# A transformer block with adaptive layer norm: one MLP part moved to the end of the program, bias sums tile by tile, and a second way to empty a PSUM bank

## The chip, the cores and the metric

The kernel runs on one core of one Trainium2 chip. The metric is the device time of the whole program in microseconds (us), lower is better. Engines are named as in the profile: PE is TensorE, DVE is VectorE, ACT is ScalarE, POOL is GpSimd, SP is the engine that issues most DMAs.

## The reference, cut to what matters

The input x has 8 sequences of 1024 tokens with 512 channels, all in float32. From a condition vector come six rows per sequence: shift, scale and gate for attention and for the MLP.

```python
mod = silu(condition) @ Wada + bada
sh_a, sc_a, gt_a, sh_m, sc_m, gt_m = jnp.split(mod, 6, axis=1)
xm = layernorm(x, g1, be1) * (1 + sc_a) + sh_a
x = x + gt_a * (causal_attention(xm, Wqkv, 16 heads) @ Wproj + bproj)
xm = layernorm(x, g2, be2) * (1 + sc_m) + sh_m
x = x + gt_m * (gelu(xm @ W1 + b1) @ W2 + b2)      # W1: 512 -> 2048, W2: 2048 -> 512
```

## The kernel before, in words

**Blocks.** The tokens are cut into 16 blocks of 512, numbered 0 to 15; an even block is the first half of a sequence, an odd one the second half. Attention of an odd block also looks at the keys of the even one before it, so it is about twice as long. Per block there are these steps of linear work on PE: `k`, `q`, `v` (projections), `proj` (output projection), `u` 0 to 3 (MLP up, four quarters) and `d` 0 to 3 (MLP down, four parts). All but `proj` use Strassen's seven products in place of eight. A down product is 64 matmuls, which the profile shows as 128 records; a product of the others is 32 records. Of the seven down products, parts 0 and 1 and part 3 have two each, part 2 has one. `mt` is not linear work: it normalizes the residual, turns it and writes the MLP's input `xm_m`; `at` does this for attention's input `xm_a`. In blocks 0, 1, 14 and 15 the turning is done by PE, in the others by DVE and DMA.

**One order, laid by a planner.** The kernel's Python runs once and writes every engine's instructions in order. It keeps an estimated clock for each engine in `now`, and due times of keys in `written` and `left`. Two streams are merged: attention (`attend`), and a list of linear steps, `plan[w]` for each window w, where window w runs beside attention of block w. `step_aside` inserts linear work ahead of an attention step if that step would wait by the planner's clocks, or if the linear work done is less than what is due. What is due grows with each attention step at a `rate`, which is the planned time of `plan[w]` over the need of the window's attention. `plan[16]` holds what runs when all attention has been placed. Threads started beside the main list (`start`) come first in the list of threads, and the first with the least wait is taken.

**The steps around the change.** In `plan[15]` the order is: part 1 of block 13, `proj` and `mt` of block 14, parts 2 and 3 of block 13, then the four up steps of block 14, its parts 0 and 1. `plan[16]` has part 2 of block 14, part 3 as a thread beside, then `proj`, `mt` and the MLP of block 15. `proj` waits until attention of its block is finished, and what stands behind it in the main list waits with it. In even windows the order is k, q, v of the next block.

**Banks and sums.** Linear products go to three PSUM banks. `copy_out` empties a bank by DVE or ACT, whichever is sooner by the clocks; `combine_out` adds the product to an earlier one and is always on DVE (line 193). `either` (lines 158 and 161) puts an SBUF sum on DVE or POOL by the clocks.

**The residual.** `load_xr` loads x for a block, and queues four jobs that add the bias row `gba` (gate times `bproj`) to its four tiles, in `pool_jobs`. These are placed when POOL is idle by its clock and the data is there; what is left is placed at the end of `project_out`. Then `bias_row(n, "m")` loads the row `gbm` into the same single buffer, by a DMA on SP's queue. `act_jobs` holds the four normalizing instructions of a block, placed when ACT or DVE is not ahead of PE by the clocks.

Of the kernel before, what the change touches and what calls it, by code (L numbers as in the profile page):

```python
# [12 lines left out]
ALU = mybir.AluOpType  # L13
# [9 lines left out]
def kernel(  # L23
# [33 lines left out]
    nc = tc.nc  # L57
# [6 lines left out]
    NTT = TB // P  # L64
# [47 lines left out]
    def note(engine, ns, reads=(), writes=(), port=False):  # L112
        start = max(now[engine], due(reads, writes))
        if port:
            start = max([start] + [b for a, b in pool_spans if a <= start < b])
        end = start + ns
        now[engine] = end
        if engine == "POOL":
            pool_spans.append((start, end))
            del pool_spans[:-16]  # L120
        for k in reads:
            left[k] = max(left.get(k, 0.0), end + SYNC)
        for k in writes:
            written[k] = end + SYNC
        return end
# [64 lines left out]
        live[bank] = not last  # L190

    def combine_out(out, bank, src, other, reads=(), writes=(), op=ALU.add, last=True):
        nc.vector.tensor_tensor(out, src, other, op)  # L193
        note("DVE", 690, [("l", bank), *reads], writes)
        live[bank] = not last

    def matmul(ps, lhsT, rhs, start, stop, reads=(), bank=None):
# [30 lines left out]
    def mlp_steps(n):  # L228
        return [("u", n, i) for i in range(NQ)] + [("d", n, part) for part in range(4)]
# [9 lines left out]
    for w in range(1, NB):  # L239
        n = w - 1  # L240
        m = mlp_steps(n)
        even = blocks[n][1] == 0
        rows_a = [("rows", blocks[n][0], "a")] if even else []
        rows_m = [("rows", blocks[n][0], "m")] if even else []
        own = m[:1] + ([("load_xa", w + 2)] if w + 2 < NB else []) + m[1:3]
        own += [("norm_a", w + 2)] if w + 2 < NB else []
        if w == NB - 1:
            steps = late[:1] + rows_a + [("proj", n), ("mt", n)] + late[1:]
            steps += rows_m + own + m[3:5] + [("load_xr", w)] + m[5:6]
            late = m[6:]  # L250
        else:

            steps = late + [("v", w)] + rows_a + [("proj", n), ("mt", n), ("k", w + 1)]
            if w > 3 and blocks[w][1]:
                steps = late[:-1] + rows_a + [("proj", n), ("mt", n)] + late[-1:] + [("k", w + 1)]
            if w == 2:
                steps = late + [("v", w), ("k", w + 1)] + rows_a + [("proj", n), ("mt", n)]
            if w == 1:
                steps = rows_a + [("k", w + 1), ("proj", n), ("mt", n)]
            early_v = [("v", w + 1)] if w > 2 and not blocks[w][1] else []  # L260
            steps += [("q", w + 1)] + early_v + rows_m + own
            at = [("at", w + 2)] if w + 2 < NB else []
            if blocks[w][1] == 0:

                steps += m[3:5] + [("load_xr", w)]
                late = m[5:6] + at + m[6:]
            else:
                steps += m[3:5] + [("load_xr", w)] + m[5:6] + at
                late = m[6:]
        plan[w] = steps  # L270
    n = NB - 1
    plan[NB] = [late[0], ("beside", late[1]), ("proj", n), ("mt", n)] + mlp_steps(n)

    kept_sums = {}
    column_source = {"k": (Wqkv, 1), "q": (Wqkv, 0), "v": (Wqkv, 2)}
# [265 lines left out]

    def run_act_jobs(everything=False):
        while act_jobs and (
            everything or (min(now["ACT"], now["DVE"]) <= now["PE"] and due(act_jobs[0][1]) <= now["PE"])
        ):
            act_jobs.pop(0)[0]()

# [469 lines left out]
    def add_to(xt, other, reads, writes, op=ALU.add):  # L1017
        either(xt, xt, other, op, [*reads, *writes], writes)

    def project_out(n):  # L1020
        at = take(NC)
        yield [("attended", n), ("xr begun", n)], []
        attT = qTs[n]
        tiles = [residual[n][:, t, :] for t in range(NTT)]
        last = n == NB - 1
        begun = []

        def begin(t):

            bank = yield from accumulate(  # L1030
                [(attT[:, c, ts(t, P)], piece(at[c])) for c in range(NC - 1)], [("att", n)], False
            )
            begun.append(bank)

        for t, xt in enumerate(tiles):
            if last:
                while len(begun) <= max(t, 1):
                    yield from begin(len(begun))
                bank = begun[t]
                yield [("att", n, t)], []  # L1040
                matmul(
                    banks[bank], attT[:, NC - 1, ts(t, P)], piece(at[NC - 1]), False, True,
                    [("att", n, t)], bank,
                )
            else:
                bank = yield from accumulate(
                    [(attT[:, c, ts(t, P)], piece(at[c])) for c in range(NC)], [("att", n)]
                )
            y = tmp.tile([P, D], F32, tag="y", name=f"y_{n}_{t}", bufs=2)
            ky = y_key("proj", True)  # L1050
            combine_out(y, bank, banks[bank], gate_rows["ga"], [("row", "ga")], [ky], ALU.mult)
            if last:
                run_pool_jobs(True)
                nc.vector.tensor_tensor(xt, xt, y, ALU.add)
                note("DVE", 700, [ky, ("xr", n, t)], [("xr", n, t)], port=True)
                following = normalize_tile(xt, f"m{n}", t, ("xr", n, t))
                if t > 0:
                    pending()
                pending = following
            else:  # L1060
                add_to(xt, y, [ky], [("xr", n, t)])
        if last:
            pending()
        release(*at)
        run_pool_jobs(True)
        bias_row(n, "m")
        if not last:
            normalize(residual[n], f"m{n}", [("xr", n, t) for t in range(NTT)])

    def up(step):  # L1070
        _, n, q = step

        def gelu():
            for i in range(NC):
                f = q * NC + i
                nc.scalar.activation(  # L1076
                    hT[:, i, :], hT[:, i, :], AF.Gelu, bias=cols[:, O_B1 + f : O_B1 + f + 1]
                )
                k = q // 2 + 1
                note_act(590, "gelu", [("h", n, q)], [(n, f"B{k}1"), (n, f"B{k}2"), ("g", n, q)])  # L1080

        def finished():
            if q == NQ - 1:
                written["m used", n] = 0.0
            excursion(gelu, [("h", n, q)], first=True)

        if (n, q) == (0, 0):
            yield ["prepared up"], []
        written["g", n, q] = NEVER
        hT = act.tile([P, NC, TB], F32, tag="hT", name=f"hT_{n}_{q}", bufs=NQ)  # L1090
        hTs[n, q] = hT

        yield from strassen(
            step,
            f"m{n}",
            lambda f, t: hT[:, half(f, 2), half(t, HB)],
            ("h", n, q),
            False,
            finished,
        )  # L1100
# [31 lines left out]
    def load_xr(n):  # L1132

        if n > 1:
            yield [("stored", n - 2)], []
        xr = xrp.tile([P, NTT, D], F32, tag="xr", name=f"xr_{n}")
        residual[n] = xr
        for t in range(2):
            nc.sync.dma_start(xr[:, half(t, 2), :], some_rows(x, n, t))
        for t in range(NTT):  # L1140
            written["xr", n, t] = now["PE"] + LANDING
        if n > 0:
            yield [("xr", n - 1, t) for t in range(NTT)], []
        bias_row(n, "a")
        row = ("row", "gba", n)
        for t in range(NTT):
            job = lambda t=t: add_to(xr[:, t, :], gate_rows["gba"], [row], [("xr", n, t)])
            pool_jobs.append((job, [("xr", n, t), row]))
        written["xr begun", n] = 0.0

    def down(n, part):
# [85 lines left out]
        if part == 0:  # L1237
            yield [("g", n, 0), ("g", n, 1), "prepared", ("row", "gbm", n)], []
            for i in range(NTT):
                add_to(residual[n][:, i, :], gate_rows["gbm"], [("row", "gbm", n)], [("xr", n, i)])  # L1240
            combine(nc.vector, "B12", "B12", "B11")
            bank, ps = yield from product("B11")
            got["u1"] = stage("p1", "p1")
# [24 lines left out]
        else:  # L1268
# [15 lines left out]
            store(n, 0)  # L1284
            for q in range(NQ):
                hTs.pop((n, q))


    def perform(step):
# [576 lines left out]
    for n in range(NB):  # L1866
        written["attended", n] = NEVER
        written["v done", n] = NEVER
        written["stored", n] = NEVER
        written["xr begun", n] = NEVER  # L1870
        written["m used", n] = NEVER
        if n > 1:
            written["free for v", n] = NEVER
        if n > 2:
            written["free for k", n] = NEVER
# [70 lines left out]
```

## Time and profile before

| | us |
|---|---|
| median of 3 runs | 3536.86 (3535.36 to 3538.43) |
| the profiled execution | 3537.37 |
| its span, first to last instruction | 3534.7 |
| PE busy | 3461.9 (98%) |
| DVE, POOL, ACT busy | 2201.4 (62%), 2054.0 (58%), 1208.4 (34%) |

The busy time of PE is a model: matmuls overlap, and a busy PE is not PE at its peak. The granted clock is TensorE's share of its full speed. A group's row gives the number of instructions, their busy time and the mean of one, then the idle time of that engine just before them and what ended it. `w,hT` marks down products, `xm_m,w` and `t_m,w` up products, `w,qT` the output projection, `w,xm_a` and `w,t_a` the v projection.

### The profile page before, as it was taken

What the parts mean: (1) busy time and instruction counts of PE and PEld (TensorE: products, weight loads), DVE (VectorE), ACT (ScalarE), POOL (GpSimd) and SP (SyncE); (2) the same over time, 40 slices, a digit from 0 to 9 for tenths busy, and PEclk for the clock granted to TensorE, in tenths of its full rate; (3) what the DMA queues carried; (4) which work ended last, traced back from release to release, by engine and by line L of the source; (5) the groups of instructions that cost most, each with busy time, mean ns of one, the idle gap of its engine ahead of it and who ended that gap; (6) DMA issues with size and microseconds to landing.
All of it is one profiled execution on the core that took longest, in us unless ns stands there. A gap on an engine that the chain in (4) does not pass through costs nothing. (4 is left out here: it accounts for less than half of the span.)

```text
span 3534.7 us, 120362 instructions
## 1 busy us (share of the span) xinstructions
PE 3461.9 (98%) x54429; PEld 1732.1 (49%) x54429; DVE 2201.4 (62%) x2438; ACT 1208.4 (34%) x1264; POOL 2054.0 (58%) x2228
## 2 busy tenths in 40 slices
PE   8999999999999999999999999999999999999999
PEld 4444445454454545445454444544555445554445
DVE  5776675565657666665566666665666756655463
ACT  2334323352233523335233442333423343223431
POOL 2666846566357663756727566375753658537560
PEclk9999999999999999999999999999999999999999
DMA  6753434435445445353453534545354545443334
GB/s 199 239 167 106 136 115 138 138 112 157 136 127 152 111 155 153 120 160 118 135 155 119 167 112 147 149 138 145 116 158 136 154 130 147 132 134 98 114 91 140
DMA packets 328195, 491.11 MB, mean 139 GB/s; under 512 B 27260, under 2 KB 177596, under 8 KB 324100
## 3 DMA queue, kind: packets, MB, share of 16 engines
q1 hardware_dynamic: 327568, 483.39, 46.1%
q8 instruction: 428, 7.01, 0.8%
q14 instruction: 83, 0.68, 0.1%
q10 hardware_dynamic: 116, 0.03, 0.0%
HBM read 425.57 MB, written 55.64 MB: 136 GB/s over the span
## 5 line engine op out<-in xcount | busy, mean ns | idle before, releaser
L1769 POOL TENSOR_TENSOR pT<-pT,pT 128x256 f32<-128x256 f32 (+3 forms) x1254 | 1214.4, 1003 | 330.0 <-PE po L1679 186.9
L1651 ACT ACTIVATE pT<-st 128x2048 f32<-128x2048 f32 x288 | 541.0, 1878 | 1059.3 <-PE st L1639 952.3
L202 PE MATMUL bank<-w,hT 128*32 128x256 f32 x14336 | 822.7, 380 | 0.5 <-issue 0.5
L1563 DVE TENSOR_REDUCE mx<-sc 128x4 f32<-128x2048 f32 (+3 forms) x381 | 658.9, 1750 | 228.1 <-PE sc L1548 222.3
L202 PEld LDWEIGHTS bank<-w,hT 128*32 128x32 f32 x14336 | 446.5, 110 | 392.7 <-issue 111.6
L202 PE MATMUL bank<-xm_m,w 128*32 128x256 f32 x8192 | 498.5, 382 | 1.6 <-ACT xm_m L750 0.8
L202 PE MATMUL bank<-t_m,w 128*32 128x256 f32 x6144 | 381.6, 380 | 0.6 <-DVE t_m L762 0.6
L1656 POOL TENSOR_SCALAR_AFFINE_SELECT pT<-pT 128x512 f32<-128x512 f32 x256 | 173.6, 696 | 342.3 <-ACT pT L1651 339.8
L202 PEld LDWEIGHTS bank<-xm_m,w 128*32 128x32 f32 x8192 | 256.2, 110 | 223.9 <-issue 56.4
L1560 DVE TENSOR_TENSOR sc<-sc,mask 128x1024 f32<-128x1024 f32 (+1 forms) x158 | 161.5, 1022 | 309.8 <-PE sc L1548 246.5
L1548 PE MATMUL sc<-kT,qT 32*128 32x512 f32 (+3 forms) x3048 | 329.4, 522 | 8.3 <-ACT pT L1651 4.4
L1679 PE MATMUL po<-pT,v 128*32 128x512 f32 (+3 forms) x3048 | 302.0, 491 | 3.8 <-POOL pT L1656 3.6
L1639 PE MATMUL st<-qT,kT 32*128 32x512 f32 (+3 forms) x3072 | 303.8, 488 | 0.0
L202 PEld LDWEIGHTS bank<-t_m,w 128*32 128x32 f32 x6144 | 189.4, 110 | 172.8 <-issue 46.9
L1718 DVE RECIPROCAL rec<-rec 128x128 f32<-128x128 f32 x256 | 227.3, 922 | 49.0 <-ACT rec L1709 49.0
L202 PE MATMUL bank<-xm_a,w 128*32 128x256 f32 x3968 | 241.7, 380 | 0.0
L202 PE MATMUL bank<-w,qT 128*32 128x512 f32 x2048 | 238.4, 599 | 1.1 <-DMA w<-in_L_cond_Wproj_dram 1.1
L1548 PEld LDWEIGHTS sc<-kT,qT 32*128 32x128 f32 x3048 | 130.3, 184 | 191.0 <-issue 94.4
L193 DVE TENSOR_TENSOR hT<-bank,u_u 128x512 f32<-128x512 f32 x192 | 130.4, 687 | 112.0 <-PE bank L202 108.8
L202 PE MATMUL bank<-t_a,w 128*32 128x256 f32 x2944 | 185.3, 381 | 1.4 <-DVE u_d L193 1.4
L1076 ACT ACTIVATE hT<-hT,cols 128x512 f32<-128x512 f32 x256 | 164.6, 711 | 47.8 <-DVE hT L193 47.2
L202 PEld LDWEIGHTS bank<-xm_a,w 128*32 128x32 f32 x3968 | 124.6, 110 | 106.4 <-issue 27.6
(227 smaller groups left out, 3386.3 us busy)
## 6 DMA issues: line engine op xcount, KB each, us to landing
w<-in_L_cond_W_dram SPq DMA_DIRECT2D x384, 256.0 KB
w<-kept_up_S SPq DMA_DIRECT2D x256, 256.0 KB
w<-kept_down_S SPq DMA_DIRECT2D x256, 256.0 KB
w<-kept_qkv_S SPq DMA_DIRECT2D x180, 256.0 KB
w<-in_L_cond_Wqkv_dram SPq DMA_DIRECT2D x147, 256.0 KB
hat_a<-in_x_dram SPq DMA_DIRECT2D x64, 256.0 KB
xr<-in_x_dram SPq DMA_DIRECT2D x32, 512.0 KB
w<-in_L_cond_Wproj_dram SPq DMA_DIRECT2D x64, 256.0 KB
```

Source lines behind the costliest of these rows:

```text
L193: nc.vector.tensor_tensor(out, src, other, op)
L202: nc.tensor.matmul(ps[r, :], columns, rhs, start=start, stop=stop, skip_group_check=True)
L1076: nc.scalar.activation(hT[:, i, :], hT[:, i, :], AF.Gelu, bias=cols[:, O_B1 + f : O_B1 + f + 1])
L1548: nc.tensor.matmul(sc[:, j, c0 : c0 + w], qTs[n][r, gg, ts(qt, P)], keys_of(n, kh)[r, gg, :w], start=True, stop=True, skip_group_check=True,)
L1560: nc.vector.tensor_tensor(place, place, shape_of.to_broadcast(place.shape), ALU.add)
L1563: nc.vector.tensor_reduce(maxima[n, gg][:, kh, qt, :], sc[:, :, c0 : c0 + w], axis=AX.X, op=ALU.max)
L1639: nc.tensor.matmul(st[:, j, c0 : c0 + w], kT[r, gg, ts(k % NTT, P)], qT[r, gg, TB - w :], start=False, stop=True, skip_group_check=True,)
L1651: nc.scalar.activation(pT[:, :, :used], st[:, :, :used], AF.Exp, scale=scale)
L1656: nc.gpsimd.affine_select(diagonal, diagonal, pattern=[[0, HPG], [1, P]], compare_op=ALU.is_ge, fill=0.0, base=0, channel_multiplier=-1,)
L1679: nc.tensor.matmul(po[r, TB - w :], v[:, k % NTT, g * P + j * hd : g * P + (j + 1) * hd], pT[:, j, c0 : c0 + w], start=(k == 0), stop=last ...
L1718: nc.vector.reciprocal(some, some)
L1769: nc.gpsimd.tensor_tensor(into, into, pT[:, j, c0 : c0 + w], ALU.add)
```

## The change

It has six edits.

1. `plan`: part 1 of block 14 moves from window 15 to `plan[16]`, ahead of part 2; part 2 of block 13 moves ahead of `proj` of block 14; in even windows from 4 on, `v` comes ahead of `q`.
2. `combine_out`: if DVE's clock is over 3.5 us behind ACT's for this product, ACT copies the bank to the output tile, and `either` adds the other term there.
3. `project_out`: ahead of each tile one of the queued bias sums is placed.
4. The load of the row `gbm` waits, as a thread, until the last sum with the row before it has been placed and is due, by the planner's clock.
5. `run_act_jobs`: jobs are placed up to 1.5 us earlier by the clocks.
6. A guard: the first up step of block 15 waits until part 3 of block 14 is placed.

```diff
     def combine_out(out, bank, src, other, reads=(), writes=(), op=ALU.add, last=True):
-        nc.vector.tensor_tensor(out, src, other, op)
-        note("DVE", 690, [("l", bank), *reads], writes)
+        ready = due([("l", bank)], writes)
+        if op is ALU.add and out is not other and max(now["DVE"], ready) > max(now["ACT"], ready) + 3500:
+            nc.scalar.copy(out, src)
+            note_act(585, None, [("l", bank)], writes)
+            either(out, out, other, op, [*reads, *writes], writes)
+        else:
+            nc.vector.tensor_tensor(out, src, other, op)
+            note("DVE", 690, [("l", bank), *reads], writes)
         live[bank] = not last
...
         if w == NB - 1:
-            steps = late[:1] + rows_a + [("proj", n), ("mt", n)] + late[1:]
-            steps += rows_m + own + m[3:5] + [("load_xr", w)] + m[5:6]
-            late = m[6:]
+            steps = late[:2] + rows_a + [("proj", n), ("mt", n)] + late[2:]
+            steps += rows_m + own + m[3:5] + [("load_xr", w)]
+            late = m[5:]
...
-            steps += [("q", w + 1)] + early_v + rows_m + own
+            steps += early_v + [("q", w + 1)] + rows_m + own
...
-    plan[NB] = [late[0], ("beside", late[1]), ("proj", n), ("mt", n)] + mlp_steps(n)
+    plan[NB] = late[:-1] + [("beside", late[-1]), ("proj", n), ("mt", n)] + mlp_steps(n)
...
     def run_act_jobs(everything=False):
         while act_jobs and (
-            everything or (min(now["ACT"], now["DVE"]) <= now["PE"] and due(act_jobs[0][1]) <= now["PE"])
+            everything or (min(now["ACT"], now["DVE"]) <= now["PE"] + 1500 and due(act_jobs[0][1]) <= now["PE"])
         ):
...
         for t, xt in enumerate(tiles):
+            if pool_jobs and not last:
+                pool_jobs.pop(0)[0]()
...
-        bias_row(n, "m")
+
+        def next_row():
+            yield ["rowgb free"], []
+            bias_row(n, "m")
+
+        written["row", "gbm", n] = NEVER
+        start(next_row())
...
+        if (n, q) == (NB - 1, 0):
+            yield [("down done", n - 1)], []
```

The key `rowgb free` is set where the last sum with a row is placed, in `load_xr` and in part 0 of `down`; `down done` is set at the end of part 3.

More of the change, by code (lines that the diff above doesn't have):

```diff
@@ L1145, in load_xr, with add @@
         row = ("row", "gba", n)
+        def add(t):
+            add_to(xr[:, t, :], gate_rows["gba"], [row], [("xr", n, t)])
+            if t == NTT - 1:
+                written["rowgb free"] = due([("xr", n, i) for i in range(NTT)])
         for t in range(NTT):
-            job = lambda t=t: add_to(xr[:, t, :], gate_rows["gba"], [row], [("xr", n, t)])
-            pool_jobs.append((job, [("xr", n, t), row]))
+            pool_jobs.append((lambda t=t: add(t), [("xr", n, t), row]))
         written["xr begun", n] = 0.0
@@ L1240, in down @@
                 add_to(residual[n][:, i, :], gate_rows["gbm"], [("row", "gbm", n)], [("xr", n, i)])
+            written["rowgb free"] = due([("xr", n, i) for i in range(NTT)])
             combine(nc.vector, "B12", "B12", "B11")
@@ L1286, in down @@
                 hTs.pop((n, q))
+            written["down done", n] = 0.0
     def perform(step):
@@ L1869 @@
         written["stored", n] = NEVER
+        written["down done", n] = NEVER
         written["xr begun", n] = NEVER
```

## The prediction

> **What bounds the kernel now.** I read the page's head first, then the waits of TensorE, then busy time by stage, and last the order of time around each hole.
>
> ```profile
> span 3534.7 us, 120362 instructions
> PE 3461.9 (98%) x54429; PEld 1732.1 (49%) x54429; DVE 2201.4 (62%) x2438; ACT 1208.4 (34%) x1264; POOL 2054.0 (58%) x2228
> ```
>
> TensorE (PE) is busy for 98% of the span, and the change alters no matmul. So time can only come from the 72.8 us in which PE idles, from the stretches in which it runs at a lower granted clock, and from how its work is interleaved. The stages show where the idle time is:
>
> ```profile
> 250.00:3400.00 3150.00, 3117.28 (x48836) 1552.54 (x48832) 1965.01 (x2133) 1111.30 (x1148) 1895.34 (x2043) 1.00 0.46 134
> 3400.00:3434.00 34.00, 26.32 (x228) 12.90 (x224) 26.51 (x47) 10.55 (x15) 8.73 (x10) 0.86 0.27 86
> ```
>
> (Columns: stretch, its length, then busy time of PE, PEld, DVE, ACT, POOL, then granted clock, DMA share, GB/s.) The long middle loses 3150 - 3117.28 = 32.7 us, 1% of it. The 34 us at the hand-over from the last attention to the last MLP lose 7.7 us, and their clock is 0.86. By time, the places worth naming are two hand-overs, first block 14 to 15, then the end:
>
> ```profile
> 3180.00:3190.00 10.00, 8.71 (x104) 2.91 (x92) 8.37 (x8) 5.57 (x5) 8.01 (x5) 1.00 0.25 82
> 3190.00:3200.00 10.00, 8.13 (x60) 2.77 (x60) 6.15 (x12) 3.32 (x3) 10.00 (x9) 1.00 0.00 0
> ...
> 3400.00:3410.00 10.00, 5.67 (x72) 2.38 (x68) 7.58 (x8) 1.88 (x1) 8.73 (x10) 0.88 0.34 105
> 3410.00:3420.00 10.00, 10.00 (x78) 4.84 (x74) 8.75 (x15) 2.36 (x3) 0.00 (x0) 0.78 0.15 54
> 3420.00:3430.00 10.00, 7.03 (x63) 3.27 (x55) 8.49 (x23) 3.49 (x8) 0.00 (x0) 1.00 0.43 127
> 3430.00:3440.00 10.00, 9.62 (x130) 5.65 (x134) 3.58 (x5) 3.99 (x6) 5.41 (x4) 0.83 0.20 59
> ```
>
> **The change, part by part.** All sums are made against the profiled execution, 3537.4 us (its span and 2.7 us around it), 0.5 us above the median of 3536.86.
>
> *One MLP part more for the end.* What it moves is priced by the group of down products:
>
> ```profile
> L202 PE MATMUL bank<-w,hT 128*32 128x256 f32 x14336 | 822.7, 380 | 0.5 <-issue 0.5
> ```
>
> That is 57.4 ns a matmul record. Part 1 has two products of 128 records, so 14.7 us of PE work, with its loads and its sums on DVE and POOL, leave the window of block 15 and stand before the last projection. What the end lacks today is just such filler. In order of time (start, length, engine, line, instruction, in brackets the idle time before it; rows between are left out):
>
> ```profile
> 3401.58 1.48 PE L202 MATMUL bank<-w,hT 128*32 128x256 f32 x24
> 3404.83 1.07 PE L1679 MATMUL po<-pT,v 128*32 128x384 f32 x16 [1.77 <-POOL pT L1656]
> 3408.41 2.39 PE L1700 MATMUL bank<-pT,ones 128*32 128x512 f32 x8 [2.50 <-POOL pT L1769]
> 3429.91 0.33 PE L740 MATMUL bank<-ident,hat_m 128*128 128x128 f32 x1 [2.63 <-ACT hat_m L663]
> ```
>
> The down products of block 14 are used up at 3403 us. From there PE waits 1.77 us for a mask and 2.50 us for sums on POOL. Then the clock falls: (1 - 0.88) x 10 + (1 - 0.78) x 10 = 3.4 us in the two stretches quoted. With work left, this first hole closes: 1.77 + 2.50 + 3.4 = 7.7 us. The part beside comes first in the list of threads when both can run, so it is spent before the last projection. The second hole (2.63 us before the transposes, and (1 - 0.83) x 10 = 1.7 us of clock) therefore stays. One bound is 0, if attention eats the kept part as filler; the other is 7.7 + 2.97 + 0.38 + 1.7 = 12.8 us, with both holes closed (idle by the windows). I take 7.7, as the end of attention is paced by POOL, which is full there, and needs no more filler than today:
>
> ```profile
> 3390.00:3400.00 10.00, 9.55 (x140) 4.21 (x136) 7.36 (x5) 5.63 (x3) 10.00 (x7) 1.00 0.18 54
> ```
> ```profile
> L161 POOL TENSOR_TENSOR hT<-hT,hT 128x1024 f32<-128x1024 f32 x30 | 79.6, 2671 | 41.9 <-DVE hT L1166 41.9
> ```
>
> It can also cost. Part 1 sums four slabs of 128x1024 by the planner's choice; on the full POOL they are 4 x 2.67 = 10.7 us of later end for attention, 3 us more than the hole is worth. The planner gives such a sum to DVE where POOL is more than a microsecond behind, so I leave this as the other bound, +3.
>
> The Trainium skill, page "TensorE: Matmul & The Clock Gate", Part 1, says that the clock falls after at least one idle window of about 3.4 us. By it the longest gap here, 2.50 us, would leave the clock alone, and the first hole would be worth 4.3 us, not 7.7. The trace shows 0.78 behind that gap, so the trace decides.
>
> *Part 2 of block 13 goes ahead of block 14's projection.* From 3181 to 3200 us PE has only attention, since the projection waits for attention 14 and stands ahead of everything else. Idle there: 1.29 + 1.87 = 3.2 us. Part 2 is one product, 7.3 us, and covers that. It then no longer covers the norm of block 14. Is that cover missed?
>
> ```profile
> 3200.38 13.92 PE L202 MATMUL bank<-w,qT 128*32 128x512 f32 x128
> 3226.18 1.09 PE L740 MATMUL bank<-ident,hat_m 128*128 128x128 f32 x8
> 3246.08 1.05 PE L202 MATMUL bank<-xm_m,w 128*32 128x256 f32 x16
> ```
>
> The last transposes end 13 us after the projection. Part 3 alone is 14.7 us, and attention runs between, so the up projection that begins at 3246 today finds its input ready. Gain 3.2; bounds 0 and 5 (an attention with fewer stalls).
>
> *v ahead of q in even windows from 4 on.* Attention asks for the next block's scores as soon as q is there. So q is finished one step later (seven products of 32 records of 59.9 ns, 13.4 us of PE), scores begin later, and the work that remains at the hand-over is richer. The worst hand-over now:
>
> ```profile
> L202 PE MATMUL bank<-w,xm_a 128*32 128x256 f32 x1984 | 118.8, 380 | 1.0 <-ACT p_v L188 1.0
> ```
> ```profile
> 934.04 0.69 DVE L193 TENSOR_TENSOR v<-bank,u_v 128x512 f32<-128x512 f32 x1 [1.03 <-PE bank L202]
> 938.75 1.22 PE L1548 MATMUL sc<-kT,qT 32*128 32x512 f32 x8 [2.42 <-DVE mx L1563]
> 940.01 2.29 DVE L1563 TENSOR_REDUCE mx<-sc 128x4 f32<-128x2048 f32 x1 [1.32 <-PE sc L1548]
> 943.29 1.22 PE L1518 MATMUL bank<-kT,qT 32*128 32x512 f32 x1 [1.63 <-DVE mx L1535]
> 947.00 3.35 PE L202 MATMUL bank<-xm_m,w 128*32 128x256 f32 x32
> ```
> ```profile
> 900.00:950.00 50.00, 45.95 (x664) 23.42 (x660) 33.15 (x40) 15.66 (x19) 18.99 (x29) 0.90 0.43 123
> ```
>
> k, q and v are done by 934, the MLP's input comes at 947, and between them PE has only scores, which DVE paces. Cost: 2.42 + 1.63 us and (1 - 0.90) x 50 = 5.0 us of clock, 9 us together. With q last, block 4's weights would still be open then. I take a third, 3 us: it is one place, and the same swap can open a hole in another window (below). Bounds: +23 (rival 2) to -9.
>
> *ScalarE clears a bank where DVE lags.* Full banks that DVE had not emptied held PE here:
>
> ```profile
> PE bank L1601 <- DVE v L193: 1.9, 1, 1.9
> PE bank L1601 <- DVE y_d L193: 1.8, 1, 1.8
> PE bank L202 <- DVE u_d L193: 1.4, 1, 1.4
> ```
> ```profile
> L188 ACT COPY p_u<-bank 128x512 f32<-128x512 f32 x53 | 31.0, 586 | 248.5 <-PE bank L202 224.6 <-issue 23.1 <-ACT mrow L1607 0.5
> L158 DVE TENSOR_TENSOR xr<-xr,y 128x512 f32<-128x512 f32 x24 | 25.1, 1047 | 1.1
> L161 POOL TENSOR_TENSOR xr<-xr,y 128x512 f32<-128x512 f32 x36 | 48.2, 1341 | 63.5 <-DVE y L193 63.4
> ```
>
> That is 5.1 us in three places. Each time the branch is taken, a bank is free after a 0.59 us copy on an engine that is busy 34%, and DVE or POOL pays an SBUF add of 1.05 or 1.34 us in place of DVE's PSUM add. Queued behind that add are the next combinations, which use its result. Thirty such cases would add 18 us to ACT and at most 40 us to POOL, both far from full over the span. Value 3 of the 5.1 us, since the planner's clocks, not the chip, choose the cases; bounds 0 to 5.1, and +3 if an add delays the next combination.
>
> *Bias tile by tile, eager ScalarE jobs, the bias row later, the guard.* In block 4 the adds still come behind the projection, and hold its statistics:
>
> ```profile
> 1074.11 1.90 PE L202 MATMUL bank<-w,qT 128*32 128x512 f32 x16
> 1078.46 2.96 POOL L161 TENSOR_TENSOR xr<-xr,row_gba 128x512 f32<-128x512 f32 x2
> 1081.17 0.68 DVE L595 BATCH_NORM_STATS2 st_m<-xr 128x6 f32<-128x512 f32 x1
> ```
> ```profile
> L202 PE MATMUL bank<-xm_m,w 128*32 128x256 f32 x8192 | 498.5, 382 | 1.6 <-ACT xm_m L750 0.8 <-ACT p_u L188 0.7
> ```
>
> The norm can start some 4 us earlier, but PE's waits for its product sum to 0.8 us only: other work covers them. Value 1 us, with what the eager jobs add; bounds 0 and 3. The row's DMA leaves SP's queue free until POOL is done with the old row. The groups of PE quoted here list no wait for a weight load, so this gives nothing. The guard asks for part 3 of block 14 before the last up projection; part 3 comes first in any case: 0.
>
> Sum: 7.7 + 3.2 + 3 + 3 + 1 = 17.9 us. The planner lays the whole order anew, and the 32.7 us of small waits in the middle are drawn again, after an order that was already a good draw: I charge 3 us, with 4 either way. 3537.4 - 15 = 3522.4, for the median 3522 us.
>
> **Rivals.**
> 1. *The kept part is eaten.* The rate of linear work in the last window falls with its plan, but work is also taken whenever attention waits. If that takes all three parts before 3403, the first hole stays and the tail term is 0. Without a gain from the swap too: 3.2 + 3 + 1 - 3 = 4 us, 3533 us. For it: today two parts beyond the plan were eaten so. Against: those covered a wait for POOL that does not grow. Chance 0.20.
> 2. *Slower: q too late.* In six windows (4 to 14) the seven score units of a new group come after q, paced by DVE: 2.29 us a unit against 1.22 us on PE (the rows at 938.75 and 940.01). Where the MLP's input is not there either, four units leave 4 x 1.07 = 4.3 us of holes and, as behind the first hole at the end, 3.4 us of low clock: 7.7 us a window. In three of six windows that is 23 us: -15 + 3 + 23 = +11, 3548 us; it decides from two windows on, where the gain is gone. For it: today's hole at 938 us is of this kind. Against: with q last the linear stream still has work when attention stalls. Chance 0.16.
> 3. *All of it.* The hole at 938 us goes wholly (6 us more) and the second hole at the end too (5 us): 3511 us. Chance 0.16.
> 4. *The branch is never taken*, as the planner's ScalarE clock lags as well: 3 us less, 3525 us, inside the forecast.
>
> **Numbers.** The forecast itself, 3515 to 3530 us, has 0.48. A measurement of this kernel can tell about 0.2%, 7.1 us, from no change. Faster by more: 0.46 of the forecast and rival 3, 0.62. Within: rival 1 and the forecast's edge, 0.21. Slower: 0.17. Rival 2 above 3541 us (0.11) and the lowest cases (0.07) are left out: 3507 to 3541 us.
>
> **What would show it.** Right: down products between the last weights of attention 15 and the last projection, no gap over 1 us before the ones matmuls, a clock of 1.00 there; down products among 3181 to 3200 us; no wait of PE for DVE over 1.5 us at a full bank. Wrong: the last down product of block 14 ahead of the ones matmuls (rival 1); gaps at scores in even windows behind DVE reductions, with the clock under 0.95 (rival 2); or a middle, 250 to 3400 us, that loses more than 33 us.

## The result, and the profile after

The changed kernel takes 3511.3 us (median of 5 runs, 3508.34 to 3514.48), the kernel before 3536.86 us: a ratio of 0.9925, 95% interval [0.9912, 0.9939], 25.6 us less. The sign is that of the forecast and the time lies in the range. It lies 11 us under the forecast, next to the third rival, and below the forecast's own 3515 to 3530 us. The profiled execution after took 3508.85 us.

The head of the page after:

```profile
span 3506.8 us, 120394 instructions
PE 3454.8 (99%) x54429; PEld 1725.7 (49%) x54429; DVE 2210.1 (63%) x2412; ACT 1216.6 (35%) x1282; POOL 2082.2 (59%) x2245
```

The matmuls are the same 54429. PE idles 52.0 us instead of 72.8, so 20.8 of the 27.9 us of span are idle time that went. The other 7.1 us are busy time. Of the stretches after 250 us in which the clock was at half, before had 10.2 us at 939, 3.4 us at 1523, then 6.8 us at 3407 and 3.4 us at 3431, and 3.9 us in the last microseconds; after has only 6.8 us at 3400 and 2.9 us in the last microseconds.

To see where it went I cut both executions some 5 us into the up products of block 3, and where PE starts those of blocks 13 and 15: nearly the same points in the work, not in time. At 250 us the two are level; the first up product of block 0 begins at 229.86 us before and at 230.11 us after. (Columns as in the prediction.) Before:

```profile
250.00:952.00 702.00, 689.69 (x10640) 337.91 (x10636) 441.11 (x479) 255.32 (x260) 434.03 (x482) 0.99 0.43 128
952.00:3081.00 2129.00, 2112.35 (x33332) 1057.93 (x33328) 1347.26 (x1476) 742.00 (x775) 1268.65 (x1370) 1.00 0.48 140
3081.00:3433.00 352.00, 340.57 (x5088) 169.10 (x5084) 202.97 (x226) 123.75 (x127) 201.39 (x200) 0.99 0.36 110
```

After, the same stretches of work:

```profile
250.00:938.00 688.00, 678.33 (x10568) 332.78 (x10560) 430.21 (x469) 252.38 (x257) 437.26 (x482) 1.00 0.45 131
938.00:3061.00 2123.00, 2116.22 (x33360) 1057.01 (x33356) 1360.51 (x1470) 750.79 (x791) 1283.39 (x1378) 1.00 0.49 140
3061.00:3405.00 344.00, 338.61 (x5124) 167.12 (x5120) 210.65 (x218) 124.64 (x130) 208.75 (x207) 0.99 0.38 113
```

The first stretch is 14 us shorter, the middle 6, the tail 8. But the work is not cut quite alike: after has 72 records of PE fewer in the first stretch (10568 for 10640), and they lie behind the cut. Idle time and clock are free of that. The idle time (length minus PE) falls from 12.3 to 9.7, from 16.7 to 6.8 and from 11.4 to 5.4 us. The half clock that went, at half its length, is 5.1, 1.7 and 1.9 us. Together that is 7.7 us in the first stretch, 11.6 in the middle and 7.9 in the tail. So some 6 of the 14 us are attention work that moved behind the cut, and the largest part of the gain lies in the middle.

At the end of the program after, by time (PE's instructions, in brackets the idle time before each):

```profile
3365.71 1.07 PE L1702 MATMUL po<-pT,v 128*32 128x512 f32 x8 [1.70 <-POOL pT L1679]
3366.59 3.64 PE L208 MATMUL bank<-w,hT 128*32 128x256 f32 x64
...
3370.91 3.20 PE L208 MATMUL bank<-w,hT 128*32 128x256 f32 x56
...
3373.93 1.06 PE L1723 MATMUL bank<-pT,ones 128*32 128x512 f32 x8
3374.79 8.83 PE L208 MATMUL bank<-w,hT 128*32 128x256 f32 x160
3383.42 13.93 PE L208 MATMUL bank<-w,qT 128*32 128x512 f32 x128
3398.17 0.33 PE L746 MATMUL bank<-ident,hat_m 128*128 128x128 f32 x1 [0.55 <-ACT hat_m L669]
3400.92 0.47 PE L746 MATMUL bank<-ident,hat_m 128*128 128x128 f32 x1 [2.42 <-ACT hat_m L669]
```

Down products (`w,hT`) lie between the last weights of attention 15 and the projection (`w,qT`), which needs no wait and runs at full clock. The 1.70 us wait for a mask stays. So does the second hole, and it now costs more clock than before, (1 - 0.66) x 10 = 3.4 us, where it was 1.7:

```profile
3390.00:3400.00 10.00, 7.94 (x74) 2.51 (x64) 9.15 (x22) 2.49 (x6) 0.00 (x0) 1.00 0.40 130
3400.00:3410.00 10.00, 8.85 (x90) 5.63 (x94) 3.53 (x8) 4.48 (x7) 3.72 (x3) 0.66 0.16 52
```

At 938 us, where before lost 9 us, one wait is left:

```profile
932.56 1.34 PE L208 MATMUL bank<-xm_m,w 128*32 128x256 f32 x16 [1.38 <-ACT xm_m L756]
```

### The profile page after: what moved, and what is told of

Same layout as the page of the kernel before. It is cut to its first block, busy times and chain, and to the rows that moved or that the text cites. A ratio compares the mean times of both kernels' runs of the same rounds, so it can differ in the third digit from the quotient of the medians.

```text
span 3506.8 us, 120394 instructions
## 1 busy us (share of the span) xinstructions
PE 3454.8 (99%) x54429; PEld 1725.7 (49%) x54429; DVE 2210.1 (63%) x2412; ACT 1216.6 (35%) x1282; POOL 2082.2 (59%) x2245
```

## Experiments: one edit alone, put on the kernel before

Theory A: the parts have each their own holes and their gains add up. Theory B: the planner's order was drawn anew by every edit, and no part has a price of its own. Each of six kernels has one group of edits on top of before. All ratios are to the kernel before, whose median lay between 3537.0 and 3539.6 us when the others were run; so ratios are compared, and gains in us are worked out from them.

**The plan of the end** (the two edits of `plan[15]` and `plan[16]`, with the guard).

```diff
-            steps = late[:1] + rows_a + [("proj", n), ("mt", n)] + late[1:]
-            steps += rows_m + own + m[3:5] + [("load_xr", w)] + m[5:6]
-            late = m[6:]
+            steps = late[:2] + rows_a + [("proj", n), ("mt", n)] + late[2:]
+            steps += rows_m + own + m[3:5] + [("load_xr", w)]
+            late = m[5:]
...
-    plan[NB] = [late[0], ("beside", late[1]), ("proj", n), ("mt", n)] + mlp_steps(n)
+    plan[NB] = late[:-1] + [("beside", late[-1]), ("proj", n), ("mt", n)] + mlp_steps(n)
```

> The kernel before with the plan edits alone: part 1 of block 14 kept for the end, part 2 of block 13 ahead of block 14's projection, and the guard. Theory A (each edit closes its own hole, and the gains add): the hand-over 14 to 15 loses its 3.2 us and the end some 5 us, so 8 us less than before (3529), with the middle up to 3160 us as before. Rival B (the planner draws the whole order anew, and the gain is a lucky draw of all edits together): the part up to 3160 us is laid by the same steps and stays as it is, so B also expects under 8 us here; if the kept part is eaten as filler, 3533 to 3537.

Measured: 3530.05 us, ratio 0.9982 [0.9973, 0.9991], about 6.4 us less. The stretch between the up products of blocks 13 and 15 is 343 us instead of 352. Of the first hole, waits of 1.70 and 0.92 us are left, with no fall of the clock; the second hole has 0.54 and 2.52 us and 6.8 us at half clock; the gaps at 14 to 15 are gone. The middle is as in before, with its hole at 938 us, but for one wait at 2657 us that grew from 1.86 to 2.27 us and has 3.4 us at half clock behind it.

**`v` ahead of `q`.**

```diff
-            steps += [("q", w + 1)] + early_v + rows_m + own
+            steps += early_v + [("q", w + 1)] + rows_m + own
```

> The kernel before with v ahead of q in even windows alone. Theory A: this edit, by letting scores begin later, closes the hole at 938 us of the kernel before (4.05 us idle and 5.1 us of clock), so 6 to 10 us less, 3528. Rival B: single edits scatter by 4 us to either side, and the hole at 938 goes only with other edits (the faster norm of block 3): 3533 to 3541.

Measured: 3534.68 us, ratio 0.9993 [0.9984, 1.0002]. At 934 us a wait of 2.15 us is left and the clock stays; the up products of block 3 begin 9 us earlier. By block 8 this is given back: the up products there begin at 1988 us in place of 1989, behind a wait of 4.10 us at 1519 us with 6.8 us at half clock (3.75 and 3.4 us before) and one of 2.14 us at 1799 us, with 3.4 us at half clock. A gain at one place, a loss at another; the total is not told from nothing.

**ScalarE clears a bank.** Only `combine_out` is changed, as in the change's diff.

> The kernel before with ScalarE's way to empty a bank alone. Theory A: the waits of PE for a bank that DVE had not emptied (1.8, 1.4, 1.9 and 1.3 us, at 404, 1100, 2658 and 604 us) go, 5 to 6 us less, 3531. Rival B: the branch is taken some 24 times, the order behind it is drawn anew, and other waits come: within 4 us of before.

Measured: 3533.73 us, ratio 0.9993 [0.9984, 1.0003]. The waits for a bank at 404, 1100 and 2658 us shrink or go, and so does one at 604 us for `mcols`, a cast on DVE. Waits of 2.73 us at 1104 and 1.59 us at 1806 us are new, and so are 3.4 us at half clock at 706 and at 1105 us. Not told from nothing either.

**Bias tile by tile, the row later, eager ScalarE jobs.** Edits 3, 4 and 5 together.

```diff
         for t, xt in enumerate(tiles):
+            if pool_jobs and not last:
+                pool_jobs.pop(0)[0]()
...
-        bias_row(n, "m")
+        def next_row():
+            yield ["rowgb free"], []
+            bias_row(n, "m")
+        written["row", "gbm", n] = NEVER
+        start(next_row())
...
-            everything or (min(now["ACT"], now["DVE"]) <= now["PE"] and due(act_jobs[0][1]) <= now["PE"])
+            everything or (min(now["ACT"], now["DVE"]) <= now["PE"] + 1500 and due(act_jobs[0][1]) <= now["PE"])
```

> The kernel before with the bias sums tile by tile, the later load of the bias row, and the eager normalizing jobs alone. Theory A: the MLP's input comes some 4 us earlier in even blocks, which PE hardly waits for: 1 to 2 us less, 3535. Rival B: scatter of 4 us either way. Rival C (the hole at 938 us is closed by the faster norm of block 3, not by the order of v and q): 8 to 10 us less, 3528, with no hole there.

Measured: 3520.9 us, ratio 0.9961 [0.9948, 0.9974]. This is the group I gave 1 us, and alone it brings some 14 us: the holes at 938 and at 1523 us are both gone. So it was cut once more.

**Eager ScalarE jobs alone** (the last line of that diff).

> The kernel before with the eager normalizing jobs alone. Theory F (placing the four normalizing instructions of a block together on ScalarE brings the MLP's input of block 3 forward by 8 us and closes the hole at 938 us, worth 9 us with its clock): 9 to 14 us less than before, 3526, no gap over 1 us between 930 and 950 us. Rival E (the bias sums do it, by starting the norm 4 us earlier in even blocks): within 3 us of before, the hole at 938 us stays.

Measured: 3526.1 us, ratio 0.9971 [0.996, 0.9982], about 10 us less. No gap is left at 938 us, and the up products of block 3 begin at 934 us instead of 947. The holes at 1089 and at 1513 us stay.

**The bias edits alone** (tile by tile and the row later, without the eager jobs).

> The kernel before with the bias sums tile by tile and the later load of the bias row alone. Theory F: 0 to 5 us less than before, with the hole at 938 us still there, and the one at 1523 us gone or not (3534). Rival E: 10 us less, 3527.

Measured: 3529.67 us, ratio 0.9979 [0.997, 0.9988], about 7.4 us less. Here the hole at 938 us stays, and those at 1100 and 1523 us go. The middle idles 10.2 us, where it was 16.7:

```profile
951.00:3073.00 2122.00, 2111.83 (x33344) 1056.61 (x33340) 1355.46 (x1479) 743.33 (x777) 1267.63 (x1365) 1.00 0.48 140
```

**How the eager jobs close the hole at 938 us.** ACT's instructions for the MLP's input of block 3, in before (only the normalizing, L636, and the modulating, L750):

```profile
904.70 0.82 ACT L636 ACTIVATE hat_m<-xr,offset_m,rstd_m 128x512 f32<-128x512 f32 x1
...
943.22 2.93 ACT L750 ACTIVATE xm_m<-hat_m,shiftm,gainm 128x512 f32<-128x512 f32 x4 [6.74 <-DMA hat_m<-held_m]
```

and with the eager jobs alone:

```profile
902.53 2.93 ACT L636 ACTIVATE hat_m<-xr,offset_m,rstd_m 128x512 f32<-128x512 f32 x4
...
930.59 2.21 ACT L750 ACTIVATE xm_m<-hat_m,shiftm,gainm 128x512 f32<-128x512 f32 x3
```

In before ACT has three of the four jobs, spread from 904.7 to 911.9 us, and the fourth is on DVE at 914.5 us; DVE's last transpose then ends at 928.8 us, and the row set is stored at 929.67 and loaded again from 935.15 us. With all four in one piece on ACT the transposes end at 913.1, the store is at 913.07 and the load at 919.45 us. The last of the jobs ended some 10 us earlier and the modulating began 13 us earlier, as a place in DVE's and in SP's order came with it. (About 2 us of both are a lead that this execution has there anyway.) The hole in PE was at its scores, 30 us behind the cause.

**How the bias edits close the hole at 1523 us.** What SP issues, in order of time, before:

```profile
1494.39 0.32 SPq L685 DMA_DIRECT2D held_a<-xm_a  x1
...
1508.89 0.34 SPq L522 DMA_DIRECT2D row_gbm<-kept_gbm  x1
1509.33 1.80 SPq L690 DMA_DIRECT2D hat_a<-held_a  x4
```

On the other engines, also before:

```profile
1505.88 2.98 POOL L161 TENSOR_TENSOR xr<-xr,row_gba 128x512 f32<-128x512 f32 x2
1518.78 2.93 ACT L750 ACTIVATE xm_a<-hat_a,shifta,gaina 128x512 f32<-128x512 f32 x4 [12.43 <-DMA hat_a<-held_a]
1521.61 1.85 ACT L1651 ACTIVATE pT<-st 128x2048 f32<-128x2048 f32 x1
1523.52 2.09 PE L1548 MATMUL sc<-kT,qT 32*128 32x512 f32 x8 [3.75 <-ACT pT L1651]
```

POOL's last sum with the old row ends at 1508.86 us, and the load of the new row (L522) is issued at 1508.89. The load of attention's input (L690) stands right behind it in the queue, though its data was stored at 1494 us. ACT waits 12.43 us for it; the exponentials (L1651) stand behind that on ACT, and PE waits 3.75 us for them, with 3.4 us at half clock after. With the bias edits alone the last sums with the old row run earlier, and SP has

```profile
1492.12 1.11 DVE L158 TENSOR_TENSOR xr<-xr,row_gba 128x512 f32<-128x512 f32 x1
1500.29 1.11 DVE L158 TENSOR_TENSOR xr<-xr,row_gba 128x512 f32<-128x512 f32 x1
```
```profile
1503.26 0.42 SPq L522 DMA_DIRECT2D row_gbm<-kept_gbm  x1
1503.78 2.64 SPq L690 DMA_DIRECT2D hat_a<-held_a  x4
```

5.5 us earlier, and the hole is gone. SP's own waits in before show the blocking over the whole program, 30.8 us in 11 waits, at six of the 16 loads of the row:

```profile
SPq L522 <- DVE xr L158: 15.7, 6, 4.2
SPq L522 <- POOL xr L161: 15.1, 5, 5.1
```

With the eager jobs alone 14.9 and 15.1 us of it remain; with the bias edits no such row is among those over 4.5 us. At 1503 us it is the earlier sums that do this: the row's load stands between the same loads in SP's queue as in before, and no longer has to wait there. What the later placing of the row adds at other places was not run apart and stays open.

The hole at 1100 us, which the prediction gave to the new branch, closes by the same edits. Before, and then the bias edits alone, the same instruction of DVE and what PE waited for:

```profile
1099.30 0.68 DVE L193 TENSOR_TENSOR u_d<-bank,u_d 128x512 f32<-128x512 f32 x1
1100.03 1.93 PE L202 MATMUL bank<-t_a,w 128*32 128x256 f32 x32 [1.38 <-DVE u_d L193]
```
```profile
1092.68 0.68 DVE L193 TENSOR_TENSOR u_d<-bank,u_d 128x512 f32<-128x512 f32 x1
```

## Experiments: one edit taken from the kernel after

Four kernels undo one group each. In these the kernel after had the ratio 0.9925.

**Without the plan of the end** (the first diff above, reversed).

> The changed kernel without its plan edits for blocks 13 and 14 (and without the guard). Theory A (gains add): 8 us above the changed kernel, 3519, the end with its first hole as in the kernel before. Rival B (a lucky draw): no fixed relation; the middle may move as well.

Measured: 3518.76 us, ratio 0.9946 [0.9931, 0.9961], 7.4 us slower than after. The first hole is back (1.77 and 2.51 us, with half clock), and so are the gaps at 14 to 15 (1.08, 0.77 and 1.10 us).

**Without `v` ahead of `q`.**

> The changed kernel with q ahead of v again. Theory A: the hole near 938 us is back, 6 to 10 us above the changed kernel, 3519. Rival C (the faster norm closes it): within 3 us of the changed kernel. Rival B: anything within 8 us either way, with no hole at that place.

Measured: 3509.77 us, ratio 0.9922 [0.9906, 0.9939]: no difference from after.

**Without the new branch of `combine_out`.**

> The changed kernel with VectorE alone emptying into sums. Theory A: waits of PE for full banks are back, 5 us above the changed kernel, 3516. Rival B: scatter, within 4 us either way, and the waits at other places.

Measured: 3514.86 us, ratio 0.9936 [0.9921, 0.995], 3.9 us slower than after, with intervals that overlap. In after the branch is taken 24 times. Two of its groups, and the wait for a bank that DVE holds which is left in PE's list (before: 5.1 us in three):

```profile
L195 ACT COPY hT<-bank 128x512 f32<-128x512 f32 x5 | 2.9, 586 | 13.6 <-PE bank L208 13.6
L195 ACT COPY u_d<-bank 128x512 f32<-128x512 f32 x4 | 2.4, 590 | 16.6 <-PE bank L208 16.6
...
PE bank L1624 <- DVE hT L199: 0.4, 1, 0.4
```

**Without the bias edits and the eager jobs.**

> The changed kernel without the bias and norm edits. Theory A: 1 to 2 us above the changed kernel, 3513. Rival C: 8 us above, with the hole at 938 us. Rival B: scatter of 4 us.

Measured: 3522.2 us, ratio 0.9955 [0.9941, 0.997], 10.6 us slower than after. 6.8 us of half clock at 936 us are back, and the fall at 1523 us too.

The sums fit theory A. By the ratios, times 3537 us, the single gains are 6.4 (end), 2.5 and 2.5 (the two undecided ones) and 13.8 us (bias and jobs together), 25.2 us in sum, against 26.5 us for all of it. Bias edits and eager jobs overlap: 7.4 + 10.3 apart, 13.8 together. Each of these figures is uncertain by some 3 to 5 us either way, so the sum alone does not rule theory B out; taken off, the four come to 20.8 us. What speaks for A is that the holes go and come back with the same edits: those at 14 to 15 and the first at the end with the plan, those at 938 and 1523 us with bias and jobs. Theory B is right of the two undecided edits, where a gain at one place came with new waits at others.

## Experiments: the last product held until the projection is placed

The tail of after still has the second hole, as its filler is spent ahead of the projection. So the last down product of block 14 is held until the projection has been placed, and then gives way to any step that can run as early.

```diff
+    beside = [None]
+    written["proj placed"] = NEVER
...
             start(perform(step[1]))
+            beside[0] = sides[-1]
...
-        advance(min(threads(), key=lambda thread: wait_of(thread[1])))
+        yields = written["proj placed"] == 0.0
+        advance(min(threads(), key=lambda thread: (wait_of(thread[1]), yields and thread is beside[0])))
...
         if last:
             pending()
+            written["proj placed"] = 0.0
...
+            if n == NB - 2:
+                yield ["proj placed"], []
             bank, ps = yield from product("B21")
```

> The changed kernel, with the last down product of block 14 held back until the last projection is placed, and then yielding to the transposes. If the wait for the norm (0.55 + 2.42 us, then 3.4 us of low clock) was open only because the kept part was spent ahead of the projection: 5 to 6 us below the changed kernel, 3506, a clock of 1.00 there. If the norm's chain gets longer because the product's sums on DVE come between (the chain is on DVE): 0 to 2 us below, or above.

Measured: 3506.88 us, ratio 0.9915 [0.9902, 0.9929]. The stretch that took 344 us in after takes about 340, and the clock stays up:

```profile
3381.30 13.93 PE L208 MATMUL bank<-w,qT 128*32 128x512 f32 x128
3395.03 1.93 PE L208 MATMUL bank<-w,hT 128*32 128x256 f32 x32
...
3397.37 0.33 PE L746 MATMUL bank<-ident,hat_m 128*128 128x128 f32 x1 [0.41 <-ACT hat_m L669]
3397.63 2.37 PE L208 MATMUL bank<-w,hT 128*32 128x256 f32 x40
```
```profile
3400.00:3410.00 10.00, 9.79 (x147) 5.59 (x151) 6.11 (x14) 5.07 (x8) 2.31 (x2) 1.00 0.47 153
```

Down products now lie between the projection and the transposes, and among these; the wait of 2.42 us is gone, and the clock of 0.66 is 1.00. For the whole program the gain over after is not shown: the intervals overlap, and the span of the profiled execution is 3506.8 us in both, as the up products of block 13 begin at 3066 us here and at 3061 us in after.

**The same with `q` ahead of `v` again.**

```diff
-            steps += early_v + [("q", w + 1)] + rows_m + own
+            steps += [("q", w + 1)] + early_v + rows_m + own
```

> The same with q ahead of v, as in the kernel before. The order of v and q was worth nothing in the changed kernel (0.9922 against 0.9925), so this should be within 3 us of the one with v first.

Measured: 3504.63 us, ratio 0.9908 [0.9895, 0.9922], the lowest median of all. Its interval overlaps those of after and of the version before it, so it is shown to beat the kernel before, not the kernel after.

## Why the prediction was right, and where its sum was not

**What bounds the kernel: right.** PE is busy 99% of the span, and what was gained is idle time and low clock, with the matmuls unchanged.

**The tail (7.7 + 3.2 us): right in mechanism, somewhat less in size.** The edits of the end bring 6.4 us put on and 7.4 us taken off. The first hole closes but for one wait of 1.70 us for POOL, which I had counted as gone: a down product stood before it and still the mask came late, so of the signs "no gap over 1 us" did not come. The gaps at 14 to 15 close. The second hole stays, as forecast, yet its clock cost rose from 1.7 to 3.4 us. That rise need not be the change's own: without `v` ahead of `q`, and without the new branch, the same hole had 3.4 us at half clock, again a cost of 1.7. Rival 1 did not come: 280 records of down products (64 + 56 + 160) lie behind the last wait for POOL.

**`v` ahead of `q` (3 us): the place was right, the price is not shown.** The hole at 938 us does shrink by this edit alone. In the change it was closed by the eager jobs already, so nothing was left for it to take: without it after is no slower. Rival 2 did not appear. In the kernel with this edit alone the wait at 1519 us is the one that before has there, for ACT behind the load of attention's input, and the wait of 2.14 us at 1799 us names the MLP's input; neither is a score paced by DVE.

**ScalarE's branch (3 us): not decided.** 2.5 us put on, 3.9 us taken off, neither told from nothing by the runs. Of the three waits that I counted, the one of 1.4 us was a bank held by an addition stuck behind other work on DVE, and the bias edits free it too. The last rival, that the branch is never taken, is wrong: 24 times.

**Bias, jobs and row (1 us): the step that failed.** They measure 10.6 to 13.8 us. I priced the norm by the wait that names its product, 0.8 us for `xm_m`, and said that other work covers it. But I had written a paragraph earlier that PE has only scores at 938 us because the MLP's input is not there. That hole of 9 us was the wait for the norm; PE's list files it under the scores, whose releaser is a reduction on DVE. And I judged the row's DMA by PE's waits for weights, without looking at what stands behind it on SP's queue: the load of attention's input. Both were to be seen in before: SP's 30.8 us behind L522, and the start of the modulating at 943 us. Rival 3's time came true by another way than rival 3 told: the hole at 938 us went but for one wait of 1.38 us, the one at the end did not, and the hole at 1523 us, which was not in the sum, went instead.

**The charge of 3 us for a new order: not shown either way.** The gains add up without it, but 3 us are within what their sum can tell.

**The time in the range: in part luck.** The term for bias and jobs was 10 to 13 us too small, and the one for the end, 7.7 + 3.2 us, some 4 us too large. The time lies 11 us below the forecast, and in the range because this made room for rival 3, whose way it did not take.

**The clock.** The Trainium skill, page "TensorE: Matmul & The Clock Gate", Part 1, has the clock fall after an idle window of about 3.4 us. In after 6.8 us of half clock begin at 3400.4 us, inside the second of two gaps of 0.55 and 2.42 us, so the weighing by the trace (7.7 and not 4.3 us) was right in kind. What the trace shows is that the fall needs no unbroken gap of that length.

## What to carry to other kernels

In an order that is written out ahead, a stall shows at the engine's next instruction and under the last releaser, not under its cause: at each hole ask what should have run there and why its input was late, and price an edit by that hole and not by the wait that bears its operand's name. Read the waits of the DMA-issuing queue like those of an engine: a load that waited for its single buffer held the loads behind it, and the loss came out 15 us later on another engine. Filler kept for the end can be laid on both sides of the last step that makes others wait: here that took the last stretch from 344 to 340 us.

## What the runs showed of the hardware

Gaps well under 3.4 us cost clock. In before one of 2.42 us at 936 us came ahead of 10.2 us at half clock, and 1.77 and 2.50 us, some 5 us from end to end, came with 6.8 us; in after 0.55 and 2.42 us came with as much. In before and after the low stretches ahead of the last microseconds were 3.4, 6.8 or 10.2 us long, whole multiples of 3.4. The same hole does not always cost the same. The first hole at the end had 6.8 us of half clock in some kernels and 3.4 us in others with the same order there. One gap of 2.15 us ahead of the same matmul (block 3, 932 us), after the same work of PE, cost no clock with `v` ahead of `q` alone and had 6.8 us at half clock behind it in the kernel without the bias edits and the eager jobs. In fourteen profiles the first up product of block 0 began between 226 and 232 us. After and the kernel without `v` ahead of `q` have the same order on every compute engine up to there, yet theirs began at 230.1 and 226.5 us; this is why single parts were compared by stretches of work and not by the whole span.
